# A two-layer graph network on one core: a fixed order for the fill, and four steps moved in the turns

## The chip, the core and the metric

The kernel runs on one core of one Trainium2 chip. The metric is the device time of one execution in microseconds (us); lower is better. Before the change it is 2993.7 us, the median of three runs (2993.65 to 2993.97).

The engines are called PE (TensorE matmuls), PEld (TensorE weight loads), DVE (VectorE), ACT (ScalarE), POOL (GpSimd) and SP (SyncE, which here only issues DMAs).

## The reference

64 graphs of 256 nodes with 256 features go through two layers. All is float32; `adj` is a 0/1 integer matrix.

```python
# layer 0
def _gat(h, adj, W, a, out_features):
    Wh = jnp.matmul(h, W)
    e = leaky_relu(Wh @ a[:out] + swapaxes(Wh @ a[out:], 1, 2), 0.2)
    att = softmax(where(adj > 0, e, NEG), axis=1)
    return att @ Wh
h = _gat(_gat(x, adj, W1, a1, F), adj, W2, a2, F)
h = _layernorm(x + h, g_ln1, b_ln1)
x = _layernorm(h + relu(h @ w_ff1 + b_ff1) @ w_ff2 + b_ff2, g_ln2, b_ln2)
# layer 1: 8 heads of 32
attn = softmax(q @ k.T / sqrt(32), axis=-1)          # q = x Wq + bq, k = x Wk + bk
out = sum(attn * (adj == r) @ (x Wv[r] + bv[r]) for r in range(4))
x = _ln(x + out @ Wo + bo, g1, beta1)
x = _ln(x + gelu(x @ W1 + b1) @ W2 + b2, g2, beta2)
```

## The kernel before

**Units and turns.** A unit is two graphs: 512 rows, held as four blocks of 128. There are 32 units. The main loop (L1566) calls `turn(u, u+1, u+2)` 32 times. A turn works on three units at once: attention and the second feed-forward of unit y (`u`), the first feed-forward of unit x (`u+1`), and both graph attentions of unit z (`u+2`). The steps of the three are interleaved by hand. Turn 30 has no z, turn 31 has neither x nor z. What must exist before turn 0, all of unit 0 up to the end of layer 0 and the graph attentions of unit 1, is made in the fill (L1531 to L1565).

**Order.** `tc.manual_schedule(engines=...)` makes the instructions of the named engines run in the order in which they are written; the scheduler places the others by its own estimate. In the fill that is PE and SP. In a turn (L1263) it is PE, SP, DVE and ACT, in turn 31 only PE and SP. [...]

**Seven products.** Matrix products of two by two blocks are done with seven block products instead of eight, with sums of blocks made before and after. A step name such as `4a` in `hidden_seven` (L870) means product 4 on half a of the hidden features. Products 1, 6, 7, 4 of a half add up in one PSUM bank (`one[h]`), products 2, 5, 3 in another (`two[h]`); after each, `taken` (L907) copies the bank to h1 on ACT if it is the first part of its block, or adds it on DVE (L909). The next product into the bank waits for that. `c`, `d`, `r` and `s` are the activations of finished blocks on ACT; `4` activates its block itself. `HiddenOut` (L959) does the same for the second matrix: `sums` on DVE (L975), `product` on PE (L989), `add` into y on DVE (L997). `Projections` (L1008) does q, k and v.

**Banks.** `bank` gives one of six PSUM banks with the tag g; two more, po and zo, belong to attention.

**Attention.** `scores(n)` makes four banks of scores for one of four quads (graph, half of the heads) and their exponentials on ACT (L1085); `masks(n)` multiplies by the adjacency on DVE (L1089, two instructions of 128x1024), `totals(n)` adds halves on DVE (L1094), `sums(n)` are the products with v (L1104) and of the totals (L1107, zo), `shares(b)` divides.

**Graph attention.** `project` (L1137) makes one 128x260 product a block (`xpp`, L741) and copies it on ACT; `first_scores` and `second_scores` transpose a column into rows (L750); a `Softmax` (L754) has `scores` (ACT L767, then DVE L769), `exp` (ACT L772), `masks` (DVE L776), `shares` and `scaled` (ACT L792). `first_sums` and `second_sums` are the products with the weights (`hpp` L801, `ygp` L812).

**Norms.** `moments` and `norm` take statistics on DVE (L827, L828) and a power on POOL (L838, L839); `offsets` is one small DVE instruction (L846); `applied_norm` runs on ACT (L856); `affine` is two DVE instructions of 128x1024 (L865 times the gain, L868 plus the shift).

**Folding.** `folding` (L624) is a generator that folds gains and shifts of the norms into the next weights: `shifted` (16 one-column products a half, L596), `joined` (four products and two, `pr`, of 512 columns; DVE steps L616 to L622), `scaled` and the sums `seven` and `seven_out` on POOL (L573 to L603). `next(fold)` runs it to its next `yield`.

**Before the fill's block**, the weights are loaded on SP, and three steps wait for such loads: DVE's subtraction on wv (L562), POOL's row additions (L651) and DVE's on brow (L656).

Of the kernel before, what the change touches and what calls it, by code (L numbers as in the profile page):

```python
# [16 lines left out]
P = 128  # L17
# [368 lines left out]
def narrow_path(  # L386
# [172 lines left out]
    wv = const.tile([P, KB, 2, F], F32, name="wv")  # L559
    for r in range(2):  # L560
        nc.sync.dma_start(wv[:, :, r, :], t_Wv[r].rearrange("(c p) f -> p c f", p=P))
    nc.vector.tensor_tensor(wv[:, :, 1, :], wv[:, :, 1, :], wv[:, :, 0, :], ALU.subtract)  # L562
    wvf = wv.rearrange("p c r f -> p c (r f)")
    w1, w2 = weight(t_W1, "w1"), weight(t_W2, "w2")
    rg3, rb3, rg4, rb4 = row(t_g1, "rg3"), row(t_be1, "rb3"), row(t_g2, "rg4"), row(t_be2, "rb4")
# [58 lines left out]
    def folding():  # L624

        shifted(wf1, range(FB // 2), lb1, bf1, "bf1")
        yield
        shifted(wf1, range(FB // 2, FB), lb1, bf1, "bf1")
        scaled(wf1, lg1)
        wf1s.extend(seven(wf1, "wf1"))  # L630
        wf2s.extend(seven_out(wf2, "wf2"))
        yield
        joined(wqk, "wqk", brow[:, 0:2])
        wqks.extend(seven(wqk, "wqk"))
        yield
        joined(wvf, "wv", brow[:, 2:4])
        wvs.extend(seven(wvf, "wv"))
        shifted(w1, range(FB // 2), lb3, b1, "b1")
        yield
        shifted(w1, range(FB // 2, FB), lb3, b1, "b1")  # L640
        scaled(w1, lg3)
        w1s.extend(seven(w1, "w1"))
        w2s.extend(seven_out(w2, "w2"))
        yield
# [2 lines left out]


    rows = work.tile([P, T, 2 * F], F32, tag="v", name="rows", bufs=1)
    for n, (rb, v) in enumerate(((rb1, g_bf2), (rb2, t_bo), (rb3, t_b2))):  # L650
        nc.gpsimd.tensor_add(rb, rb, row(v, None, rows[:, n, :F]))  # L651
# [4 lines left out]
    nc.vector.tensor_tensor(brow[:, 3], brow[:, 3], brow[:, 2], ALU.subtract)  # L656


    mark = {}
# [94 lines left out]
    class Softmax:  # L754

        def __init__(s, u, l, wh, rows, c):
            s.u, s.wh, s.rows, s.c = u, wh, rows, c
            s.s = (work.tile([P, T, N], F32, tag="v", name=f"s{u}_{l}", bufs=1) if u > 1 else
                   work.tile([P, 2 * T, N], F32, tag="e", name=f"s{u}_{l}")[:, :T])
            s.z = work.tile([P, T], F32, tag="z", name=f"z{u}_{l}")  # L760

# [97 lines left out]
    def affine(y, g_, b_):  # L859

        times(y, g_)
        plus(y, b_)
# [355 lines left out]
    def turn(y_, x_, z):  # L1218
# [45 lines left out]
                                            ("PE", "SP", "DVE", "Activation")[:4 if X else 2]})  # L1264
        with order:
            p.sums()
            while late:
                affine(*late.pop(0))
            if X:
                n = X.pop("n")  # L1270
                offsets(*n)
# [44 lines left out]
            if X:  # L1316
                totals(0)
            else:
                with behind("projected"):
                    masks(0)  # L1320
                    totals(0)
            p("v3 q4 v4" if middle else "q4 v4")
            if waiting:
                last = norm(w, 3, wy, mv=last)
# [23 lines left out]
            if not X:  # L1348
                with behind("out"):
                    shares(0)  # L1350
            first("2b ra 1b")
            masks(2, (0,))
            first("7a")
            masks(2, (2,))
            first("5b sa 6b 4a")
            totals(2)
            first("3b rb 7b")
# [43 lines left out]
            if Z:  # L1401
                out(1)
                Z["m"].scores(0)
                Z["m"].scores(1)
                Z["m"].exp(0)
                Z["m"].exp(1)
                out.sums(4)
                offsets(*n)
                out(2)
                applied_norm(y, *n, range(T))  # L1410
                Z["m"].masks(0)
                out(5)
                Z["m"].masks(1)
                Z["m"].shares()
            elif X:
                out.product(5)
                out.sums(3)
                out.add(5)
            if not Z:
                applied_norm(y, *n)  # L1420
            else:
                Z["m"].scaled(WH)
            if Z:
                out.product(6)
                hT = normed_features(y_, 2, y, copied=(1, 2))
                nc.scalar.activation(work.tile([P, 1], F32, tag="ve", name=f"ve{y_}"), mhalf[:, 0:1], AF.Gelu)
                out.add(6)
                out.sums(3)
                out(3)
            elif X:  # L1430
                out(6)
                out.sums(4)
                out(7, 3)
            if not Z:
# [25 lines left out]
            if Z:  # L1460
                second("2a 1a")
                n = norm(x_, 1, X["y"], mv=n, rest=range(NB + 1, T))
                second("2b 1b ca 6a")
                offsets(*n)
                applied_norm(X["y"], *n, [0])
                applied_norm(X["y"], *n, [2, 3], True)
                second("5a")
                applied_norm(X["y"], *n, [1])
                affine(y, rg3, rb3)
                second("6b 5b cb")  # L1470
                X["hT"] = normed_features(x_, 1, X["y"], natural=True)
# [56 lines left out]

    waiting, late = [], []

    with tc.manual_schedule(engines={mybir.EngineType.PE, mybir.EngineType.SP}):  # L1531
        for stage in (early_first, project, first_softmax):
            stage(0)
        early_first(1)
        next(fold)
        for stage in (project, first_softmax):
            stage(1)
        first_sums(0)
        next(fold)
        second_softmax(0)  # L1540
        first_sums(1)
        next(fold)
        second_softmax(1)
        for b in range(G):
            second_sums(0, (b,))
            normed(0, 0, g[0]["y"], range(b * NB, (b + 1) * NB))
        next(fold)
        g[0]["hT"] = to_features(g[0]["y"], "h1T0")
        for u in range(2):
            checked(u, g[u]["aq"])  # L1550
        affine(g[0]["y"], rg1, rb1)
        load_x(2)
        load_rows(2)
        load_adjacency(2)
        first_hidden(0)("2a 1a 2b 1b 5a 5b 3a 3b 6a ra 6b rb 7a sa 7b sb 4a 4b")
        first = HiddenOut(0, 0, g[0]["y"], g[0]["h1"], wf2s, out_sums(0, 0))
        first.sums(1, 2, 4, 3)
        first(1, 2, 5, 6, 3)
        normed(0, 1, g[0]["y"], range(NB))
        first(7, 4)  # L1560
        normed(0, 1, g[0]["y"], range(NB, T))
        g[1]["n"] = norm(1, 0, g[1]["y"], mv=second_sums(1))
        g[0]["hT"] = with_ones(to_features(g[0]["y"], "h2T0", (nc.scalar.copy,) * 2))
        late.append((g[0]["y"], rg2, rb2))
        next(fold)  # L1565
        for u in range(NG):  # L1566
            turn(u, u + 1, u + 2)

# [53 lines left out]
```

## Time and profile before

| | |
|---|---|
| median of three runs | 2993.7 us |
| the profiled execution | 2993.49 us |
| its span, first to last instruction | 2991.8 us |
| PE busy | 2950.5 us (99%), 22192 matmuls |
| DVE busy | 2616.8 us (87%), 5024 instructions |
| ACT busy | 1820.6 us (61%) |
| POOL busy | 624.3 us (21%) |
| HBM traffic | 56.8 MB read, 16.8 MB written |

The execution's time is 1.7 us longer than its span. The page gives, for each engine, busy time, groups of instructions by line, and what ended the idle time before them; a tile's name stands without its number, so `h1a` is `one[h]` and `h1b` is `two[h]` of the hidden products. In the timeline a line starts with the start and the length of an instruction (or of several merged ones, xcount) in us; a bracket at the end gives the idle time of that engine just before it and who ended it. Matmul ends are modelled.

### The profile page before, as it was taken

To read this page: it belongs to the slowest core of one execution; us is meant where nothing else is said; L and a number is where in the kernel's file an instruction comes from. 1 tells how busy PE (TensorE), PEld (TensorE's weight loads), DVE (VectorE), ACT (ScalarE), POOL (GpSimd) and SP (SyncE) were. 2 spreads that over 40 slices of the span, in tenths; PEclk is the share of its full clock that TensorE was granted. 3 is DMA by queue.
4 is the path that set the end of the run, shared out by engine and by line. 5 is a ranking of instruction groups with operands and counts; after the bars stand their busy time and mean duration, and the time that the engine had idled before them with its cause. 6 is when DMAs were issued, how large, how long until landed. Compare 5 with 4: busy or idle time off the path is not lost.

```text
span 2991.8 us, 58459 instructions
## 1 busy us (share of the span) xinstructions
PE 2950.5 (99%) x22192; PEld 2494.1 (83%) x22192; DVE 2616.8 (87%) x5024; ACT 1820.6 (61%) x3803; POOL 624.3 (21%) x930
## 2 busy tenths in 40 slices
PE   7999999999999999999999999999999999999998
PEld 5788888888888888888888888888888888888876
DVE  5789989889898889898889898898988898988887
ACT  4466656656655666666666566566566666666653
POOL 4222111221211221211221112212112212112211
PEclk8999999999999999999999999999999999999999
DMA  5011111111111111111111111111111111111000
GB/s 150 13 29 36 34 36 26 42 34 36 33 31 33 42 34 36 30 27 40 36 37 34 35 26 42 35 37 34 31 33 42 34 36 31 26 40 35 18 11 16
DMA packets 416883, 105.36 MB, mean 35 GB/s; under 512 B 360746, under 2 KB 416084, under 8 KB 416596
## 3 DMA queue, kind: packets, MB, share of 16 engines
q1 hardware_dynamic: 415196, 100.23, 15.3%
q8 instruction: 177, 2.90, 0.4%
q0 software_dynamic: 1056, 1.05, 0.1%
q14 instruction: 110, 0.90, 0.1%
q10 hardware_dynamic: 344, 0.28, 0.0%
HBM read 56.78 MB, written 16.78 MB: 25 GB/s over the span
## 4 chain that ended last, share of the span: by engine, by line
PE 95%; DVE 2%; DMA 1%; ACT 1%; POOL 0%; issue 0%; SPq 0%; DVEq 0%; POOLq 0%; ACTq 0%
PE yf L989 26%; PE h1a L900 15%; PE h1b L900 11%; PE po L1104 8%; PE v L1056 7%; PE qk L1056 6%; PE sp L1076 5%; PE xpp L741 4%; PE yop L812 4%; PE hpp L801 3%; PE ygp L812 3%; PE zo L1107 2%; PE rows L750 1%; DVE st L827 0%; DMA wf<-in_L_gnn_w_ff_dram 0%
## 5 line engine op out<-in xcount | busy, mean ns | idle before, releaser
L1089 DVE TENSOR_TENSOR ea<-e,aT 128x1024 f32<-128x1024 f32 x256 | 307.5, 1213 | 2.8 <-ACT e L1085 2.8
L856 ACT ACTIVATE y<-y,nm,rs 128x256 f32<-128x256 f32 x450 | 242.7, 593 | 95.5 <-DVE nm L846 89.2
L912 ACT COPY h<-h1b 128x512 f32<-128x512 f32 x262 | 153.0, 584 | 223.1 <-PE h1b L900 221.4
L1085 ACT ACTIVATE e<-sp 128x512 f32<-128x512 f32 x512 | 270.8, 598 | 27.4 <-PE sp L1076 20.7
L1043 ACT COPY qk<-qk 128x512 f32<-128x512 f32 x128 | 74.5, 582 | 290.1 <-PE qk L1056 290.1
L918 ACT ACTIVATE h<-h,cols 128x256 f32<-128x256 f32 x512 | 221.7, 501 | 38.5 <-DVE h L909 38.5
L711 POOL COPY hT<-yt 32x256 f32<-32x256 f32 x244 | 211.7, 867 | 139.5 <-DVE yt L694 131.7
L909 DVE TENSOR_TENSOR h<-h1a,h 128x512 f32<-128x512 f32 x262 | 176.1, 681 | 68.3 <-PE h1a L900 64.0
L838 POOL TENSOR_SCALAR rs<-mv 128x4 f32<-128x4 f32 (+1 forms) x134 | 34.2, 255 | 897.8 <-DVE mv L828 480.1
L827 DVE BATCH_NORM_STATS2 st<-y 128x6 f32<-128x256 f32 x512 | 208.0, 408 | 5.6
L997 DVE TENSOR_TENSOR y<-yf,y 128x256 f32<-128x256 f32 x448 | 184.8, 413 | 25.5 <-PE yf L989 25.4
L1117 POOL TENSOR_TENSOR low<-low,rq 128x16 f32<-128x16 f32 x64 | 14.0, 219 | 806.9 <-DVE rq L1116 806.9
L868 DVE TENSOR_TENSOR y<-y,rb 128x1024 f32<-128x1024 f32 (+1 forms) x130 | 167.0, 1285 | 3.2
L743 ACT COPY xp<-xpp 128x260 f32<-128x260 f32 x128 | 45.5, 387 | 194.2 <-PE xpp L741 194.1
L865 DVE TENSOR_TENSOR y<-y,rg 128x1024 f32<-128x1024 f32 (+1 forms) x130 | 155.7, 1198 | 1.2 <-ACT y L856 1.1
L1094 DVE TENSOR_TENSOR es<-e 128x1024 f32<-128x1024 f32 x128 | 155.6, 1216 | 0.0
L839 POOL TENSOR_TENSOR rs<-rs,mhalf 128x4 f32<-128x4 f32 (+1 forms) x134 | 146.2, 1091 | 8.3
L1076 PE MATMUL sp<-qk 32*128 32x256 f32 x2048 | 146.6, 400 | 0.0
L1104 PE MATMUL po<-e,v 128*32 128x256 f32 x2048 | 136.3, 384 | 0.0
L900 PE MATMUL h1a<-tt,wf 128*128 128x256 f32 x512 | 134.5, 386 | 0.3 <-DVE h L909 0.3
L1104 PE MATMUL po<-ea,v 128*32 128x256 f32 x2048 | 134.3, 379 | 0.0
L741 PE MATMUL xpp<-gwe,xT 128*128 128x260 f32 x512 | 128.0, 394 | 2.8 <-ACT xT L675 2.8
(284 smaller groups left out, 7744.3 us busy)
## 6 DMA issues: line engine op xcount, KB each, us to landing
hT<-yt SPq DMA_DIRECT2D x852, 32.0 KB, 1.9
y<-in_x_dram SPq DMA_DIRECT2D x32, 512.0 KB, 4.5
xq<-in_x_dram SPq DMA_DIRECT2D x240, 64.0 KB, 2.2
aq<-in_adj_dram SPq DMA_DIRECT2D x240, 64.0 KB, 2.4
out_dram<-y SPq DMA_DIRECT2D x30, 512.0 KB, 2.8
wf<-in_L_gnn_w_ff_dram SPq DMA_DIRECT2D x2, 1024.0 KB, 7.4
w<-in_L_gnn_W_dram SPq DMA_DIRECT2D x2, 1024.0 KB, 7.6
first<-in_adj_dram POOLq DMA_DIRECT2D x2, 512.0 KB, 7.8
```

The lines of the kernel that those rows point to most:

```text
L711: nc.gpsimd.tensor_copy(to, at)
L741: nc.tensor.matmul(ps[:, :WX], hT[k][:, t * P:(t + 1) * P], gwe[:, k, :], start=(k == 0), stop=(k == KB - 1))
L812: nc.tensor.matmul(ps[:, i * F:(i + 1) * F], lhs(t, k), rhs(b, k), start=(k == 0), stop=(k == n - 1))
L856: mark["normed"] = nc.scalar.activation(y[:, t, :], y[:, t, :], AF.Identity, bias=nm[:, t:t + 1], scale=rs[:, t:t + 1])
L900: nc.tensor.matmul(ps[:, i * N:(i + 1) * N], w_[:, f * P:(f + 1) * P], m, start=first and i == 0, stop=True, skip_group_check=True)
L918: nc.scalar.activation(y, y if ps is None else ps[:, i * N:(i + 1) * N], func, bias=bi[:, f:f + 1])
L989: nc.tensor.matmul(s.ps[n][:, i * F2:(i + 1) * F2], a[:, k, i * P:(i + 1) * P], w_[:, k, :], start=n in (1, 2, 5) and i == 0 and k == 0, s ...
L1056: nc.tensor.matmul(ps[:, i * N:(i + 1) * N], l, r, start=n in (1, 2, 5) and i == 0, stop=True, skip_group_check=True)
L1076: nc.tensor.matmul(ps[a][:, j * N:(j + 1) * N], k_[hp, m, j0:j0 + P], q[hp, m, b * N:(b + 1) * N], start=True, stop=True)
L1085: nc.scalar.activation(e[:, a, :], ps[a], AF.Exp, scale=isd)
L1089: nc.vector.tensor_tensor(ea[:, a:a + 2, :], e[:, a:a + 2, :], ab[:, None, :].to_broadcast([P, 2, NB * N]), ALU.mult)
L1104: nc.tensor.matmul(po[hp, m * N:(m + 1) * N], vs[:, hp], w[:, a, j * N:(j + 1) * N], start=(n == 0), stop=(n == len(terms) - 1))
```

## The change

**Fill.** The block now orders all five engines. The order in it is new: unit 0's first softmax is complete before unit 1's adjacency and features are used; unit 0's second scores and softmax come right after its first sums; unit 1's projection, first softmax and the folding are set between. Unit 1's second softmax moves into the steps of unit 0's first hidden product. `checked` of unit 0 comes earlier. The folding has its yields elsewhere: both halves of `shifted` go together, and `seven_out` of wf2, `joined` of wqk, `seven` of wqk with `joined` of wv, and `seven` of wv are steps of their own. The three steps ahead of the block (wv, brow, the row additions) move into it. Unit 1's second scores get a buffer with the tag q. The scheme of norms splits: statistics first, `applied_norm` later.

**Turns.** The affine steps in `late` (turn 0: one; turn 31: two) move from the start of the turn to after `totals(0)`. `masks(2)`, which was two halves around step 7a, comes whole after 7a (turns 0 to 30). In turn 30, `out(6)` moves ahead of `applied_norm`, and the affine step and the store of the waiting unit move from before the second hidden product to after its steps 5a and 5b.

```diff
-    nc.vector.tensor_tensor(wv[:, :, 1, :], wv[:, :, 1, :], wv[:, :, 0, :], ALU.subtract)
...
     def folding():
         shifted(wf1, range(FB // 2), lb1, bf1, "bf1")
-        yield
         shifted(wf1, range(FB // 2, FB), lb1, bf1, "bf1")
         scaled(wf1, lg1)
         wf1s.extend(seven(wf1, "wf1"))
+        yield
         wf2s.extend(seven_out(wf2, "wf2"))
         yield
         joined(wqk, "wqk", brow[:, 0:2])
+        yield
         wqks.extend(seven(wqk, "wqk"))
+        nc.vector.tensor_tensor(brow[:, 3], brow[:, 3], brow[:, 2], ALU.subtract)
+        nc.vector.tensor_tensor(wv[:, :, 1, :], wv[:, :, 1, :], wv[:, :, 0, :], ALU.subtract)
+        joined(wvf, "wv", brow[:, 2:4])
         yield
-        joined(wvf, "wv", brow[:, 2:4])
+        for rb, v in shifts:
+            nc.gpsimd.tensor_add(rb, rb, v)
         wvs.extend(seven(wvf, "wv"))
+        yield
         shifted(w1, range(FB // 2), lb3, b1, "b1")
-        yield
         shifted(w1, range(FB // 2, FB), lb3, b1, "b1")
...
-            s.s = (work.tile([P, T, N], F32, tag="v", name=f"s{u}_{l}", bufs=1) if u > 1 else
+            s.s = (work.tile([P, T, N], F32, tag="v" if u > 1 else "q", name=f"s{u}_{l}", bufs=1)
+                   if u > 1 or u + l == 2 else
...
             p.sums()
-            while late:
-                affine(*late.pop(0))
...
                     totals(0)
+            while late:
+                affine(*late.pop(0))
             p("v3 q4 v4" if middle else "q4 v4")
...
-            first("2b ra 1b")
-            masks(2, (0,))
-            first("7a")
-            masks(2, (2,))
+            first("2b ra 1b 7a")
+            masks(2)
             first("5b sa 6b 4a")
...
+            if X and not Z:
+                out(6)
             if not Z:
                 applied_norm(y, *n)
...
             elif X:
-                out(6)
                 out.sums(4)
...
-            if waiting:
+            if waiting and Z:
                 affine(waiting[0][1], rg4, rb4)
                 stored(*waiting.pop(), slice(0, T))
...
                 second("5a 5b")
+                if waiting:
+                    affine(waiting[0][1], rg4, rb4)
+                    stored(*waiting.pop(), slice(0, T))
...
-    with tc.manual_schedule(engines={mybir.EngineType.PE, mybir.EngineType.SP}):
+    with tc.manual_schedule(engines={getattr(mybir.EngineType, n) for n in
+                                     ("PE", "SP", "DVE", "Activation", "Pool")}):
+        a, b = g[0], g[1]
...
+        early_first(0)
+        project(0)
+        first_scores(0)
+        spread(a["m"])
+        powers(a["m"])
+        early_first(1)
+        shared(a["m"])
+        a["m"].scaled(WH)
+        checked(0, a["aq"])
+        next(fold)
+        first_sums(0)
+        project(1, range(NB))
+        second_scores(0)
+        project(1, range(NB, T))
+        spread(a["m"])
+        powers(a["m"])
+        first_scores(1)
+        spread(b["m"])
+        shared(a["m"])
+        a["m"].scaled(F)
+        powers(b["m"])
+        next(fold)
+        next(fold)
+        shared(b["m"])
+        b["m"].scaled(WH)
+        parts = []
+        for k in range(G):
+            second_sums(0, (k,))
+            parts.append(norm(0, 0, a["y"], range(k * NB, (k + 1) * NB)))
+        first_sums(1)
+        next(fold)
+        for n in parts:
+            applied_norm(a["y"], *n)
+        checked(1, b["aq"])
+        a["hT"] = to_features(a["y"], "h1T0")
+        next(fold)
...
+        steps = first_hidden(0)
+        steps("2a 1a 2b 1b")
+        second_scores(1)
+        spread(b["m"])
+        next(fold)
+        steps("5a 5b")
+        powers(b["m"])
+        affine(a["y"], rg1, rb1)
+        steps("3a 3b")
+        shared(b["m"])
+        steps("6a ra 6b rb")
+        b["m"].scaled(F)
+        steps("7a sa 7b sb 4a 4b")
...
+        first(7)
+        applied_norm(a["y"], *n)
+        first(4)
+        n = norm(0, 1, a["y"], range(NB, T))
+        mv = second_sums(1)
+        applied_norm(a["y"], *n)
+        b["n"] = norm(1, 0, b["y"], mv=mv)
+        a["hT"] = with_ones(to_features(a["y"], "h2T0", (nc.scalar.copy,) * 2))
+        late.append((a["y"], rg2, rb2))
```

Here `spread` is `m.scores(0), m.scores(1)`, `powers` is `m.exp(0), m.exp(1)`, and `shared` is `m.masks(0), m.masks(1), m.shares()`.

More of the change, by code (lines that the diff above doesn't have):

```diff
@@ L649, in narrow_path @@
     rows = work.tile([P, T, 2 * F], F32, tag="v", name="rows", bufs=1)
-    for n, (rb, v) in enumerate(((rb1, g_bf2), (rb2, t_bo), (rb3, t_b2))):
-        nc.gpsimd.tensor_add(rb, rb, row(v, None, rows[:, n, :F]))
+    shifts = [(rb, row(v, None, rows[:, n, :F]))
+              for n, (rb, v) in enumerate(((rb1, g_bf2), (rb2, t_bo), (rb3, t_b2)))]
     brow = rows[one, :, F:]
@@ L655, in narrow_path @@
     nc.sync.dma_start(brow[:, 2:4], t_bv[0:2].rearrange("(o r) f -> o r f", o=1))
-    nc.vector.tensor_tensor(brow[:, 3], brow[:, 3], brow[:, 2], ALU.subtract)
     mark = {}
@@ L1529, in narrow_path, with spread, powers, shared @@
     waiting, late = [], []
-    with tc.manual_schedule(engines={mybir.EngineType.PE, mybir.EngineType.SP}):
-        for stage in (early_first, project, first_softmax):
-            stage(0)
+    with tc.manual_schedule(engines={getattr(mybir.EngineType, n) for n in
+                                     ("PE", "SP", "DVE", "Activation", "Pool")}):
+        a, b = g[0], g[1]
+        def spread(m):
+            m.scores(0)
+            m.scores(1)
+        def powers(m):
+            m.exp(0)
+            m.exp(1)
+        def shared(m):
+            m.masks(0)
+            m.masks(1)
+            m.shares()
+        early_first(0)
[3 more added lines that the diff above has]
+        powers(a["m"])
         early_first(1)
+        shared(a["m"])
+        a["m"].scaled(WH)
+        checked(0, a["aq"])
         next(fold)
-        for stage in (project, first_softmax):
-            stage(1)
         first_sums(0)
-        next(fold)
-        second_softmax(0)
+        project(1, range(NB))
[8 more added lines that the diff above has]
+        powers(b["m"])
+        next(fold)
+        next(fold)
[5 more added lines that the diff above has]
+            parts.append(norm(0, 0, a["y"], range(k * NB, (k + 1) * NB)))
         first_sums(1)
         next(fold)
[L1543 to L1546, printed above, removed]
+        for n in parts:
+            applied_norm(a["y"], *n)
+        checked(1, b["aq"])
+        a["hT"] = to_features(a["y"], "h1T0")
         next(fold)
[L1548 to L1551, printed above, removed]
         load_x(2)
@@ L1554, in narrow_path @@
         load_adjacency(2)
-        first_hidden(0)("2a 1a 2b 1b 5a 5b 3a 3b 6a ra 6b rb 7a sa 7b sb 4a 4b")
-        first = HiddenOut(0, 0, g[0]["y"], g[0]["h1"], wf2s, out_sums(0, 0))
+        steps = first_hidden(0)
[11 more added lines that the diff above has]
+        steps("7a sa 7b sb 4a 4b")
+        first = HiddenOut(0, 0, a["y"], a["h1"], wf2s, out_sums(0, 0))
         first.sums(1, 2, 4, 3)
         first(1, 2, 5, 6, 3)
[L1559 to L1565, printed above, removed]
+        n = norm(0, 1, a["y"], range(NB))
+        first(7)
[7 more added lines that the diff above has]
+        late.append((a["y"], rg2, rb2))
+    with tc.manual_schedule(engines={mybir.EngineType.PE, mybir.EngineType.SP}):
         for u in range(NG):
```

## The prediction, made before the changed kernel was seen

> **What bounds the kernel now.** I read the page's chain of waits first, then the waits of TensorE, then its busy time by stage, and last the timeline of one turn.
>
> ```profile
> PE 95%; DVE 2%; DMA 1%; ACT 1%; POOL 0%; issue 0%; SPq 0%; DVEq 0%; POOLq 0%; ACTq 0%
> ```
>
> ```profile
> 0.00:112.00 112.00, 89.98 (x447) 73.29 (x447) 61.55 (x141) 46.67 (x100) 42.67 (x55) 0.89 0.36 100
> 112.00:2863.00 2751.00, 2750.59 (x20856) 2331.18 (x20857) 2458.43 (x4708) 1722.49 (x3603) 567.28 (x848) 1.00 0.16 34
> 2863.00:2991.80 128.80, 109.92 (x891) 89.60 (x889) 96.82 (x177) 51.42 (x102) 14.37 (x28) 0.97 0.04 14
> ```
>
> The numbers before the first brackets are PE's busy us, the third from last the granted clock. TensorE is never idle for long between 112 and 2863 us; only the fill (22 us idle, clock 0.89) and the drain (19 us idle) are open. So the fill's rewrite can win at most some 20 us, and anything that touches the 31 turns with a partner unit counts thirty times. A busy row still hides stalls, so I looked at one turn (29 periods from turn 0 to turn 29 take 2631.9 us, 90.75 each).
>
> ```profile
> 2767.98 0.69 DVE L909 TENSOR_TENSOR h<-h1a,h 128x512 f32<-128x512 f32 x1 [0.62 <-PE h1a L900]
> 2768.59 1.22 DVE L1089 TENSOR_TENSOR ea<-e,aT 128x1024 f32<-128x1024 f32 x1
> 2769.72 0.68 DVE L909 TENSOR_TENSOR h<-h1a,h 128x512 f32<-128x512 f32 x1
> 2770.32 1.22 DVE L1089 TENSOR_TENSOR ea<-e,aT 128x1024 f32<-128x1024 f32 x1
> 2771.45 1.22 DVE L1094 TENSOR_TENSOR es<-e 128x1024 f32<-128x1024 f32 x1
> 2772.59 0.68 DVE L909 TENSOR_TENSOR h<-h1b,h 128x512 f32<-128x512 f32 x1
> ...
> 2769.22 0.84 PEld L900 LDWEIGHTS h1a<-tt,wf1s 128*128 128x128 f32 x4
> 2770.45 0.73 PEld L900 LDWEIGHTS h1a<-tt,wf 128*128 128x128 f32 x4 [0.40 <-DVE h L909]
> 2771.21 0.84 PEld L900 LDWEIGHTS h1b<-hT,wf1s 128*128 128x128 f32 x4
> ```
>
> Here step 4a loads its weights 0.40 us late, because the addition of step 7a (2769.72) stands behind half a mask (2768.59) on VectorE. A group of four normally takes 0.864 us (the chain of waits gives 1.73 for eight); from 6b to 3b two groups take 2771.21 - 2769.22 = 1.99 us, so the stall costs 1.99 - 1.73 = 0.26 us.
>
> A second wait in the same turn shows no loss at all, but is at its limit:
>
> ```profile
> 2773.30 1.33 ACT L943 ACTIVATE h<-h,cols 128x512 f32<-128x512 f32 x2 [0.75 <-DVE h L909]
> 2774.55 0.58 ACT L1085 ACTIVATE e<-sp 128x512 f32<-128x512 f32 x1
> ...
> 2775.17 0.19 PEld L741 LDWEIGHTS xpp<-gwe,xT 128*128 128x128 f32 x1
> ```
>
> The line at 2775.17 is the first load of the second projection block (`project`, t=1). It starts 0.05 us after the first exponential of `scores(3)` ends (2775.12). The g tag has six banks: four hold `scores(3)`, one the open product of half b, one the first projection block; the second block needs the bank that the first exponential frees. That exponential stands behind `rb` (L943), which waits for 3b's addition (2772.59).
>
> **The Trainium skill.** "TensorE: Matmul & The Clock Gate", Architectural detail, says that TensorE's queue pulls weight loads ahead of running matmuls, while ScalarE and VectorE are strictly first in, first out. The trace agrees: the load at 2775.17 was 0.09 us behind its place (4 x 0.219 after 2774.32 + 0.11 for the cold first) and cost nothing. After the stall at 2770.45 the next group came 0.76 instead of 0.864 later: a load may be about 0.11 us late for free. The same page, Part 1 (What's actually happening), says TensorE falls to half clock after about 3.4 us of little activity; here the clock was 0.50 from 62.7 to 73.0 us. "SBUF — State Buffer", Who interferes with whom, has VectorE and GpSimd share a port pair under an exclusive lock: the same addition took 2.02 us at 108.15 beside GpSimd's weight scaling and 1.23 at 2775.21 without.
>
> **The turns: one edit.** `masks(2)` whole after 7a. Nothing is added or removed; VectorE's order becomes 1b, 7a, mask, mask, totals, 3b, 7b.
> - 7a's addition is ready when 7a's last matmul ends, 2768.73, plus 0.04 as for 7b: 2768.77. It ends by 2769.5, 4a's load is due at 2770.08: the stall goes, -0.26 us.
> - VectorE is free after 1b's addition at 2768.59 and now waits to 2768.77: 0.18 us that the half mask used to fill. Everything behind it in order (masks, totals, 3b's addition, then `rb` and the exponentials on ScalarE) is 0.18 later: the first exponential ends at 2775.31, the second block's load starts at 2775.36. Its place, 0.26 earlier now, is 2774.82. The load is 0.54 late, 0.11 of it free; its matmul starts at 2775.36 + 0.11 = 2775.46 instead of 2775.30.
> - Net +0.16 us a turn, in the 30 turns that project a third unit: **+4.9 us**. If 7a's addition has a second wait in front (1b's started 0.11 after its matmul, not 0.04), +0.23 a turn, +7.0 in all. If the bank isn't the limit, -0.26 a turn, -8 in all.
>
> After 2775.46 nothing waits: VectorE catches up before 7b (3b's addition then ends at 2773.4), so masks(3) is 0.03 later against a TensorE that is 0.16 later.
>
> **The fill, laid out queue by queue with durations of the trace** (scores 0.39 a row, L769 0.65, exponential 0.63, L776 0.35, scaling 0.42, projection or aggregation block 0.86, `joined` 1.73 + 0.86, one `shifted` 1.84; GpSimd 1.27 a fold operation).
> - Gains: VectorE no longer stands 6.5 us at the wv transfer (L562), so the first softmax's exponentials start at 23.0, not 24.98; unit 0's second softmax starts at about 37.4 instead of 42.25. `h1T0` follows at about 61.5, and 2a at about 64.7 instead of 67.55: -2.8 us at that point.
> - Losses inside that stretch: unit 0's masks are queued behind unit 1's L769, and `joined`'s small product behind both; TensorE stands from about 39.5 to 44.4 and goes cold. Unit 0's offsets stand behind wv's folding on VectorE, to 60.4. GpSimd, in order too, holds wf2's folding back for unit 0's second shares (34 to 44) and then runs it beside unit 1's masks, which I lengthen by 1 us; the three row additions (1.0 each) come at about 58, long before their first use at 75. Unit 1's second scores, now in tag q, are free again after its `ygp`, before turn 0's first copy. SP's order is the same, and no DMA is added.
> - Afterwards: before, 2a to turn 0's q5 took 111.96 - 67.55 = 44.4 us. Now 0.44 (rows of unit 1) and one more `shifted` (1.84) stand in it, and two `shifted` in a row are 3.7 us of one-column matmuls, after which I take the clock as halved for 5a to 3a (+2.5). ScalarE must do unit 1's exponentials before 3a's copy, and its four scalings (1.7) before sa, sb and the ends of 4a and 4b; these end at about 90, so yf2 starts there, 1.8 us idle behind yf1. The last offset of unit 0 stands behind the second `ygp` addition. Turn 0's q1 starts at about 108.0 instead of 103.8.
> - Turn 0 gains back: no affine step of 3.2 us (1.25 + 1.94) and no slow L846 (1.22) ahead of q's addition, so q5 doesn't wait (2.83 before), and GpSimd's folding is done. Four steps are 3.45 warm, 4.7 cold: q5 at 111.5 to 112.7, against 111.96. The moved affine step delays unit 1's differences by 1.6 us; 1.7 us of gaps before 1b's addition (1.10 + 0.62) take that up.
>
> Sum for the fill: **+0.4 us**, from -3 (clock stays up, no port conflicts) to +4 (masks and affine steps each locked out by GpSimd).
>
> **The drain, turn 30.**
>
> ```profile
> PE yf L989 <- DVE y L997: 3.5, 3, 1.5
> PE h1b L900 <- DVE tt L882: 1.4, 1, 1.4
> PE h1a L900 <- DVE h L909: 0.9, 2, 0.8
> ```
>
> `out(6)` ahead of the norm: its addition goes at 2882.1 instead of 2882.62, behind no offset that waits for GpSimd: -0.5. The affine step of the waiting unit leaves the queue ahead of the differences (tt): the 1.4 us wait and its 0.1 restart go. The offsets come earlier too, so 3a's copy isn't behind a late norm on ScalarE: most of the 0.8 goes, as does part of ScalarE's tail, which turn 31's first copies wait for (2908.47). The 4a gain of this turn is nothing, since zo waits for totals(3) there. Its store is some 5 us later, last on SP until the outputs of turn 31, with a free y buffer meanwhile, so no one waits. The two late steps in turn 31 are not in a fixed order there; I price them at 0 (-0.5 to +1), under VectorE's 2.8 us gap at 2914. Sum **-3.2**, from -4.5 to -1.
>
> **Sum.** 4.9 + 0.4 - 3.2 = +2.1 us on the profiled execution's 2993.49 (span 2991.8 and 1.7 around it): 2995.6; the median shown is 2993.7, so 2996.
>
> **Rivals.**
> - The bank isn't the limit (0.10): another bank is free for the second block. For it: the wait costs nothing today. Against: it follows the exponential's end by 0.05 us, and I count no seventh bank. -8 + 0.4 - 3.2: 2983.
> - The fill works as meant (0.15): TensorE stays warm, gaps are filled, -6 instead of +0.4: 2989.
> - Slower (0.20): the fixed order in the fill. ScalarE's queue from 5a to 4b holds unit 1's exponentials and scalings ahead of the copies and activations that free TensorE's banks; each further microsecond there is one at q1. It costs +6 to +8 instead of +0.4: about 3001. It decides from a fill later by 4.3 us.
>
> **Numbers.** A measurement of this kernel can tell about 0.2% (6.0 us) from no change. The likeliest case (0.55) runs from 2991 to 3000. Range 2988 to 3002: below lie the first rival and the tail of the second (0.13), above the tail of the third (0.07). Faster by over 0.2%: 0.10 + 0.04; slower: most of the third and a tail of the likeliest, 0.23; the rest, 0.63, within.
>
> **What would show it.** 4a's load without a wait in each turn, and a new one of about 0.5 us on L741 behind the exponential, with turns of 90.9 us: right; turns of 90.5: the first rival. q5 of turn 0 near 112 and TensorE idle behind yf1 near 88 to 90 show the fill; tt without a wait in turn 30 shows the drain. A fill outside -3 to +4, or turns other than 90.9, would make it wrong.

## The result and the profile after

The changed kernel takes 3002.1 us, the median of 12 runs (2999.24 to 3003.2), beside 2994.5 us for the kernel before in the same session: a ratio of 1.0022, 95% interval 1.0013 to 1.0031. That is 6 us more than the 2996 of the prediction and just above the upper end of its range (3002). By the medians the change costs 7.6 us, by the ratio 6.6, where the prediction had +2.3 on its base of 2993.7.

The profiled execution took 2999.24 us, the shortest of the 12; its span is 2997.6 us against 2991.8 before, +5.8 us. I profiled the same kernel once more (run e11); that execution has a span of 3001.1 us and stands for the longer runs. The table cuts the traces at the first q matmul of each turn, all in us.

| | before | predicted change | after | after, again |
|---|---|---|---|---|
| turn 0 starts (q1) | 103.78 | +4.2 | 110.36 | 112.52 |
| turn 0 lasts | 96.15 | -3.6 | 91.84 | 91.85 |
| turns 1 to 29 last | 2631.88 | +4.7 | 2636.09 | 2636.24 |
| of these an undisturbed turn | 90.73 | +0.16 | 90.90 | 90.90 |
| turn 30 lasts | 73.46 | -3.2 | 72.50 | 74.18 |
| turn 31 to the end | 86.57 | 0 | 86.80 | 86.30 |

Both are executions at the short end of their kernel's runs. Four differences of the first profile make up its +5.8: fill and turn 0 +2.27 (q1 6.58 later, turn 0 4.31 shorter), the turns +4.21 (29 times 0.17, less 0.6 for two turns of the trace before that were 0.3 us longer than the others), turn 30 -0.96, the end +0.23.

The chain of waits and the busy time by stage of the changed kernel:

```profile
PE 89%; DVE 7%; ACT 2%; issue 2%; POOL 0%; DMA 0%; ACTq 0%; DVEq 0%; POOLq 0%
```

```profile
0.00:112.00 112.00, 88.49 (x438) 71.70 (x439) 57.70 (x135) 45.16 (x97) 44.33 (x57) 0.89 0.35 100
112.00:2863.00 2751.00, 2745.96 (x20838) 2329.16 (x20837) 2457.28 (x4707) 1715.31 (x3597) 566.14 (x845) 1.00 0.16 34
```

VectorE's part of the chain rose from 2% to 7%: each turn now hangs on an exponential that follows VectorE's masks and additions (in e12 below, without that wait, it is 2% again). PE is busy for 2745.96 of 2751 us in the middle; it was 2750.59. The missing 4.6 us have one name among TensorE's waits over the whole span:

```profile
PE h1a L904 <- DVE h L913: 5.9, 3, 3.7
PE xpp L744 <- ACT e L1089: 5.0, 30, 0.2
```

The second line is the wait that the prediction named, thirty times 0.17 us; the three waits of the first lie in the fill (3.7) and in turn 30. The turn that was shown before, in the changed kernel:

```profile
2774.28 0.69 DVE L913 TENSOR_TENSOR h<-h1a,h 128x512 f32<-128x512 f32 x1 [0.62 <-PE h1a L904]
2775.08 0.69 DVE L913 TENSOR_TENSOR h<-h1a,h 128x512 f32<-128x512 f32 x1
2775.68 1.22 DVE L1093 TENSOR_TENSOR ea<-e,aT 128x1024 f32<-128x1024 f32 x1
...
2776.39 0.84 PEld L904 LDWEIGHTS h1a<-tt,wf 128*128 128x128 f32 x4
...
2781.05 0.57 ACT L1089 ACTIVATE e<-sp 128x512 f32<-128x512 f32 x1
...
2781.67 0.30 PEld L744 LDWEIGHTS xpp<-gwe,xT 128*128 128x128 f32 x2 [0.57 <-ACT e L1089]
```

7a's addition (2775.08) now stands ahead of the mask, and 4a's load (2776.39) has no bracket any more: that stall is gone. The first exponential of `scores(3)` ends at 2781.62, the second block's load starts 0.05 us behind it, and its bracket gives 0.57 us of idle time. Some 0.03 of that lies between any two groups of loads (as in e12 below), so the load is 0.54 us late.

### The profile page after: what moved, and what is told of

It reads as the page before. It is cut to its first block, busy times and chain, and to the rows that moved or that the text cites. A ratio compares the mean times of both kernels' runs of the same rounds, so it can differ in the third digit from the quotient of the medians.

```text
span 2997.6 us, 58472 instructions
## 1 busy us (share of the span) xinstructions
PE 2950.6 (98%) x22192; PEld 2496.0 (83%) x22192; DVE 2617.6 (87%) x5024; ACT 1816.1 (61%) x3803; POOL 624.8 (21%) x930
## 4 chain that ended last, share of the span: by engine, by line
PE 89%; DVE 7%; ACT 2%; issue 2%; POOL 0%; DMA 0%; ACTq 0%; DVEq 0%; POOLq 0%
PE yf L993 26%; PE h1a L904 12%; PE h1b L904 9%; PE po L1108 8%; PE v L1060 7%; PE qk L1060 6%; PE hpp L805 4%; PE yop L816 4%; PE ygp L816 4%; PE sp L1080 3%; PE xpp L744 3%; DVE ea L1093 2%; PE zo L1111 2%; DVE h L913 2%; PE rows L753 1%
```

## The experiments

Each is an edit of the kernel before or of the changed one; every run has a profile and a ratio to the kernel before. The stages of all of them, cut as above:

| run | q1 | turn 0 | a turn | turn 30 | turn 31 | span | ratio to before, 95% |
|---|---|---|---|---|---|---|---|
| before | 103.78 | 96.15 | 90.73 | 73.46 | 86.57 | 2991.8 | |
| e1 | 104.08 | 96.34 | 90.90 | 73.48 | 87.10 | 2997.6 | 1.0015 (1.0008 to 1.0021) |
| e2 | 110.42 | 91.68 | 90.73 | 72.48 | 86.55 | 2992.3 | 1.0003 (0.9995 to 1.0011) |
| e3 | 103.61 | 95.91 | 90.47 | 73.47 | 86.57 | 2983.5 | 0.9973 (0.9963 to 0.9984) |
| e12 | 110.92 | 91.41 | 90.47 | 74.08 | 86.33 | 2986.5 | 0.9979 (0.9971 to 0.9987) |
| e4 | 108.01 | 96.56 | 90.90 | 72.50 | 86.87 | 3000.3 | 1.0022 (1.0013 to 1.0031) |
| e5 | 107.64 | 91.85 | 90.90 | 74.17 | 86.27 | 2996.0 | 1.0012 (1.0004 to 1.0020) |
| e6 | 103.55 | 92.74 | 90.73 | 73.46 | 86.66 | 2988.1 | 0.9985 (0.9978 to 0.9991) |
| e7 | 103.67 | 98.51 | 90.73 | 72.99 | 86.63 | 2993.7 | 0.9997 (0.9988 to 1.0005) |
| e8 | 103.91 | 92.49 | 90.47 | 70.42 | 92.28 | 2983.0 | 0.9961 (0.9948 to 0.9975) |
| e9 | 103.18 | 93.08 | 90.47 | 70.42 | 86.36 | 2976.8 | 0.9948 (0.9935 to 0.9962) |
| e10 | 107.02 | 93.01 | 90.47 | 70.42 | 86.16 | 2980.2 | 0.9954 (0.9940 to 0.9968) |

### The turns: e1, e2, e3 and e12

e1 makes the one edit of the turn alone, in the kernel before:

```diff
-            first("2b ra 1b")
-            masks(2, (0,))
-            first("7a")
-            masks(2, (2,))
+            first("2b ra 1b 7a")
+            masks(2)
```

> The kernel before with one edit, the whole of masks(2) behind step 7a. Bank theory: 4a's stall of 0.26 us goes, the second projection block waits for the first exponential of scores(3), a turn takes 90.90 us instead of 90.73, in 30 turns +5.1 us against before; fill and drain as before. Rival, the longer turn of the changed kernel comes from the state that its fill leaves (buffers, order of the DMAs): turns of 90.73, no change. Rival, the bank is no limit: turns of 90.47, -7.8 us.

Turns of 90.90 us, a span 5.7 us longer and a median 4.4 us longer (2999.21 against 2994.83): the edit alone brings the whole loss of the turns, with the old fill and the old drain around it, and TensorE waits thirty times for the exponential, 5.2 us in all. Both rivals fall.

e2 is the reverse edit in the changed kernel.

> The changed kernel with the old order of masks(2), half of it ahead of step 7a. Bank theory: turns of 90.73 us again, -5 us against the changed kernel, and what is left against before is the fill (+2.3 at the end of turn 0) and the drain (-1.0), so +1 us against before. Rival, the turn was lengthened by something else in the change: turns stay at 90.90, +5.8 us against before.

Turns of 90.73. What is left of the change is a span of 2992.3, +0.5 us (turn 0 ends at 202.10, +2.17, and turn 30 is 0.98 shorter), and a median 1.2 us longer (2996.03 against 2994.83), which its interval doesn't tell from no change. The turns' cost is wholly in this edit.

e3 asks whether the bank is the cause. It keeps the edit and lets the second projection block need its bank one step later:

```diff
-                project(z, range(0, T // 2))
+                project(z, (0,))
             first("4b")
+            if Z:
+                project(z, (1,))
```

> The kernel before with masks(2) behind step 7a and the second projection block behind step 4b instead of ahead of it, so that it needs its bank 0.86 us later. Bank theory: the exponential has ended by then, only the 4a stall is removed, turns of 90.47 us, -7.8 us against before. Rival, the wait moves on to the next thing (step 4b itself waits for 7b's addition, or sums(2) or masks(3) for the later exponentials): turns of 90.7 to 90.9, 0 to +5 us.

Turns of 90.47, so 4a's 0.26 us are now a gain and nothing takes their place; 7.8 us were expected against before, the median is 7.76 us lower (2987.07 against 2994.83). So it was the place of this block that made it wait; it doesn't read what the exponential writes, and by the program the bank is what joins the two. e12 makes the same edit in the changed kernel.

> The changed kernel with one edit: the second projection block behind step 4b. Bank theory: turns of 90.47 instead of 90.90, 0.43 in each of 30 turns, -12.9 us against the changed kernel, the span about 2984.7, -7 us against before. Rival, in the changed kernel another wait (its xpp copy on ScalarE behind 4b's activations) takes the bank's place: turns of 90.7, -6 us.

Turns of 90.47 there too, -0.43 each. The loads of the two blocks in e12:

```profile
2768.59 0.74 PEld L744 LDWEIGHTS xpp<-gwe,xT 128*128 128x128 f32 x4 [0.33 <-issue]
2769.36 0.84 PEld L904 LDWEIGHTS h1a<-tt,wf 128*128 128x128 f32 x4
2770.22 0.84 PEld L744 LDWEIGHTS xpp<-gwe,xT 128*128 128x128 f32 x4
```

The second block's load (2770.22) follows 4b's (2769.36) with no wait for the exponential. One line of order makes the same edit cost 5 us or gain 8.

### The fill: e4, e5 and e6

In the changed kernel q1 came at 110.36, where 108.0 was predicted. Its timeline at that place:

```profile
76.07 1.95 DVE L872 TENSOR_TENSOR y<-y,rb 128x1024 f32<-128x1024 f32 x1
77.94 1.49 DVE L780 SCALAR_TENSOR_TENSOR s<-s,aT 128x256 f32<-128x256 f32 x1
...
83.78 1.27 DVE L913 TENSOR_TENSOR h<-h1a,h 128x512 f32<-128x512 f32 x2
...
80.64 1.32 POOL L574 TENSOR_TENSOR w1s<-w,w1s 128x512 f32<-128x512 f32 x1
81.92 1.44 POOL L575 TENSOR_TENSOR w<-w 128x512 f32<-128x512 f32 x1
...
84.60 5.38 PE L904 MATMUL h1a<-tt,wf 128*128 128x256 f32 x16 [3.73 <-DVE h L913]
```

The four masks of unit 1's second softmax (L780, from 77.94 to 83.65) take 1.48 us each beside GpSimd's folding of w1, and 6a's addition (83.78) is queued behind them, so TensorE stands for 3.73 us. e4 moves the GpSimd operations away, to the end of the fill:

```diff
+        yield
         scaled(w1, lg3)
         w1s.extend(seven(w1, "w1"))
...
         late.append((a["y"], rg2, rb2))
+        next(fold)
```

> The changed kernel with GpSimd's ten operations on w1 and w2 moved from the middle of the fill to its end, the rest unchanged. Port theory: the four masks of the partner unit take 0.35 to 0.42 us each instead of 1.48, the two affine operations 1.22 instead of 1.96, TensorE no longer stands 3.7 us for 6a's addition, q1 of turn 0 at about 106.6 instead of 110.4 us; turn 0 then has the folding beside its first additions and gives back about 1.5 us, so -2 us against the changed kernel. Rival, the masks are slow for another reason (their operands, the read of the accumulator): they stay at 1.48 and q1 at 110.4, no change.

```profile
79.49 0.42 DVE L781 SCALAR_TENSOR_TENSOR s<-s,aT 128x256 f32<-128x256 f32 x1 [2.15 <-ACT s L777]
...
81.42 0.69 DVE L914 TENSOR_TENSOR h<-h1a,h 128x512 f32<-128x512 f32 x1 [0.25 <-PE h1a L905]
...
124.39 4.50 POOL L715 COPY hT<-yt 32x256 f32<-32x256 f32 x4
...
128.94 1.13 PE L905 MATMUL h1b<-hT,wf 128*128 128x256 f32 x4 [2.60 <-POOL hT L715]
```

A mask takes 0.42 us, 6a's addition starts as soon as its matmul has ended, and q1 comes at 108.01. So the slow masks come from GpSimd's work beside them, as the lock would have it. But the gain (2.35 us at q1) was smaller than expected, since a stretch of halved clock lay beside it (the 8 matmuls of step 5 took 3.76 us instead of 2.68), and turn 0 gave back 4.72 us where I had expected 1.5: the folding now runs from 109 to 124 us, and in GpSimd's queue its copies of unit 1's features (124.39) wait behind it; step 2a stands 2.60 us for them, and a half-clock stretch from 130.2 to 133.6 us follows right behind. The span is 2.7 us longer than in the first profile of the changed kernel, but that was the shortest of its runs: the medians, 3001.76 and 3002.14, and the ratios show no difference. The folding at the end wins nothing.

e5 leaves the folding where it is and moves the masks out of its way, behind additions of the output product:

```diff
-        shared(b["m"])
         steps("6a ra 6b rb")
-        b["m"].scaled(F)
...
-        first(1, 2, 5, 6, 3)
+        first(1, 2, 5)
+        b["m"].masks(0)
+        first(6)
+        b["m"].masks(1)
+        b["m"].shares()
+        b["m"].scaled(F)
+        first(3)
```

> The changed kernel with the second masks of unit 1 (and the four scalings after them) moved in the fill from between steps 3b and 6a to between the additions of the output product of unit 0; GpSimd's folding stays where it is. Queue theory: 6a's addition is no longer behind slow masks, TensorE doesn't stand 3.7 us there, q1 of turn 0 at about 108.0 instead of 110.4 us as with the folding at the end, but turn 0 keeps its 91.84: -2.3 us against the changed kernel. Rival, 6a's addition is itself slowed by GpSimd (1.5 us each instead of 0.69) and the stall is only spread over 6a to 7b: q1 at 110, no change.

q1 comes at 107.64 and turn 0 keeps its 91.85: the queue theory holds, and turn 0 ends 2.7 us earlier than in the changed kernel. (Turn 30 was 1.67 longer in this trace; e11 explains why.) Its timeline shows who GpSimd locks out and who not:

```profile
81.18 0.69 DVE L913 TENSOR_TENSOR h<-h1a,h 128x512 f32<-128x512 f32 x1 [0.17 <-PE h1a L904]
...
86.99 2.17 DVE L979 TENSOR_TENSOR eq<-eq,h 128x1024 f32<-128x1024 f32 x1
89.27 2.10 DVE L979 TENSOR_TENSOR eaq<-h,eq 128x1024 f32<-128x1024 f32 x1
...
92.99 2.02 PE L993 MATMUL yf<-wf2t,eq 128*128 128x128 f32 x16 [2.60 <-DVE y L1001]
```

The additions of the hidden product, which take one operand from PSUM, need 0.69 us with GpSimd busy as without. The sums of the output product, both operands in SBUF, need up to 2.17 us instead of 1.22, and the next wait (2.60) is already there: the output additions are queued behind four sums, three of them slowed. The Trainium skill, "SBUF — State Buffer", Who interferes with whom, says that a VectorE instruction with two SBUF inputs contends with a GpSimd instruction that reads SBUF, and one with at most one SBUF input, outside the modes that use both ports, doesn't. The durations here agree on both halves of that.

e6 takes the late affine step of turn 0 alone, in the kernel before:

```diff
             p.sums()
-            while late:
-                affine(*late.pop(0))
...
+            while late:
+                affine(*late.pop(0))
             p("v3 q4 v4" if middle else "q4 v4")
```

> The kernel before with the late affine step alone moved behind totals(0). As predicted: q5 of turn 0 doesn't wait 2.83 us for q's addition, turn 0 takes about 93.3 us instead of 96.15, and turn 31 is unchanged: -2.8 us against before. Rival: GpSimd's queue still holds the folding ahead of its copies of unit 1's features, as in the kernel with the folding at the end, and the first step of unit 1 (2a) waits for them instead: turn 0 stays at 95.5 to 96.5, no change.

Turn 0 takes 92.74 us, -3.41, turn 31 is as before, and the median is 2990.15 against 2995.0. The wait of q5 before, and in e6:

```profile
PE qk L1056 <- DVE qk L1040: 2.8, 1, 2.8
PE qk L1056 <- DVE qk L1040: 0.6, 2, 0.5
```

So most of the 4.31 us that turn 0 won in the changed kernel come from this move of two instructions, which needs no new fill. (The trace before has a half-clock stretch at q1, from 103.7 to 107.1 us, and e6 has none; e9 below, with such a stretch, has 93.08, -3.07.)

### The drain: e7, e8, e9 and e10

e7 makes the move of the waiting unit's affine step alone.

```diff
-            if waiting:
+            if waiting and Z:
                 affine(waiting[0][1], rg4, rb4)
                 stored(*waiting.pop(), slice(0, T))
...
                 second("5a 5b")
+                if waiting:
+                    affine(waiting[0][1], rg4, rb4)
+                    stored(*waiting.pop(), slice(0, T))
```

> The kernel before with the affine step and store of the waiting unit alone moved in turn 30 from ahead of the differences to behind step 5b. As predicted: the 1.4 us wait for the differences and most of the 0.8 us wait go, turn 30 takes 71.3 us instead of 73.46. Rival: the two operations of 1.22 us now stand ahead of the offsets, so the norm on ScalarE and with it 3a's copy and 6a's addition come later, and TensorE waits 2 us for 6a's addition: turn 30 takes 73.4 to 73.6, no change.

Turn 30 takes 72.99 us, -0.47: nearer to the rival than to the prediction. (Turn 0 is 2.36 longer in this trace with nothing changed there; a stretch of halved clock from 110.0 to 116.9 us lies on it.) The changed kernel shows what happens, in turn 30:

```profile
2901.82 1.22 DVE L869 TENSOR_TENSOR y<-y,rg 128x1024 f32<-128x1024 f32 x1
2903.07 1.22 DVE L872 TENSOR_TENSOR y<-y,rb 128x1024 f32<-128x1024 f32 x1
2904.21 0.15 DVE L850 SCALAR_TENSOR_TENSOR nm<-mv,rs 128x4 f32<-128x4 f32 x1
2905.51 0.69 DVE L913 TENSOR_TENSOR h<-h1a,h 128x512 f32<-128x512 f32 x1 [1.14 <-ACT h L916]
...
2904.40 0.60 ACT L860 ACTIVATE y<-y,nm,rs 128x256 f32<-128x256 f32 x1 [3.03 <-DVE nm L850]
2904.91 0.56 ACT L916 COPY h<-h1b 128x512 f32<-128x512 f32 x1
...
2906.25 2.10 PE L904 MATMUL h1a<-tt,w 128*128 128x256 f32 x8 [1.97 <-DVE h L913]
```

The two moved operations (2901.82 to 2904.29) stand ahead of the offsets (2904.21), ScalarE's norm waits 3.03 us for these, 3a's copy is behind the norm, 6a's addition behind the copy, and TensorE stands 1.97 us. The wait for the differences (1.4) is gone and this one (0.8 before) has grown by 1.2.

e8 puts the gains together on the kernel before and holds the waiting unit's affine step and store over to turn 31 (only this part and the late steps' new place are shown):

```diff
+            if waiting and not Z:
+                late.append((waiting[0][1], rg4, rb4))
+                held.append(waiting.pop())
...
+            with ExitStack() if X else behind("projected"):
+                while late:
+                    affine(*late.pop(0))
+                while held:
+                    stored(*held.pop(), slice(0, T))
```

> The kernel before (its fill unchanged) with masks(2) behind 7a and the second projection block behind 4b, the late affine step behind totals(0), out(6) ahead of the norm in turn 30, and the affine step and store of the waiting unit held over to turn 31, where all late affine steps start only behind the last addition of the projections. If the costs are separate: turns of 90.47, turn 30 at 70.9 to 71.4 instead of 73.46, turn 31 shorter by about 1.2 (the wait of step 5 for q's addition goes), in all -11 to -12 us against before, a span of about 2980. Rival, the drain's gains are taken back by the sums of out and the masks of turn 31, which VectorE then does later: a span of 2983.

Turn 30 takes 70.42, -3.04, about what the prediction had asked of the drain. Turn 31 takes 92.28, +5.7: six affine operations of 1.2 us now stand ahead of `scores(1)`'s masks and between them, TensorE waits 3.3 us for these, and a stretch of halved clock (2916.4 to 2923.3) follows. The rival was right in kind.

e9 places the held step behind 7b's addition of turn 31, and the other late steps of that turn behind the first two additions of the projections.

> The kernel before, with its own fill, and the parts that gained: masks(2) behind 7a with the second projection block behind 4b; the late affine step behind totals(0), in turn 31 behind the first two additions of the projections; out(6) ahead of the norm; the affine step and store of the waiting unit held over to turn 31, behind 7b's addition there. If the terms add up: turn 0 ends at 195.9, turns of 90.47, turn 30 about 70.5, turn 31 about 85.4 (its 1.27 us wait gone), a span of 2975 to 2976, -16 us against before. Rival: the held step stands ahead of the last sums of turn 31 and the output product waits for it, turn 31 about 87.5, a span of 2978; or a stretch of halved clock falls into turn 31 as in the last kernel and adds 1.7 to 3.4 us.

Turn 31 takes 86.36, and the kernel 2978.8 us against 2994.05: a ratio of 0.9948, the fastest of all here. Of turn 31's expected 1.2 only 0.2 came; I did not follow where the rest went.

e10 is the same with the new fill, its masks as in e5 and its sums spread between the output additions.

> The changed kernel with the same mended turns and drain, and its fill mended: unit 1's masks between the additions of the output product, and the sums of that product spread between its additions, so that the additions don't wait behind four sums (2.60 us in the kernel with the masks behind). If the port lock and the queue order are what the new fill lost by: q1 of turn 0 at 105 to 105.5, turn 0 ends at about 196.4, a span of about 2976, the same as with the old fill within 1 us. Rival, the new fill order is worth less than the old whatever is mended: turn 0 ends at 198 to 199, a span of 2978 to 2979.

q1 comes at 107.02, turn 0 ends at 200.03 against 196.25 in e9, which is past even the rival's 198 to 199. Spreading the sums did remove the wait (from the first output product to q1 20.61 us instead of 22.77 in e5), but TensorE reached that product 1.54 us later than in e5, behind a half-clock stretch of 6.8 us (72.8 to 79.6; 3.4 in e5), and had another from 106.9 to 110.3 us. So part of the 3.8 us is clock, and this profile is one of the longer of five runs: the medians, 2980.49 and 2978.8, differ by 1.7 us. The new order of the fill has no lead over the old one in any of these runs; by how much it is worse once mended is not shown.

### The spread of the runs: e11

> The changed kernel, unedited, profiled once more: its profiled execution took 2999.24 us, the lowest of its runs, while their median is 3002.1. Clock theory: waits of about 2 us of TensorE (6a in turn 30, the fill's 3.7) bring a stretch of halved clock of 3.4 us or not, by where they fall against the clock's own steps, and one more such stretch costs 1.7 us; a profile near 3001 to 3002 shows one more stretch than the first, with turns of 90.90 as in the first. Rival, the turns themselves vary: a later profile near 3002 has turns longer than 90.90.

The second profile has the same turns, 90.90. It is 3.5 us longer in two places: q1 comes 2.16 later, and turn 30 takes 74.18 instead of 72.50. Busy times by window around turn 30's wait for 6a, first the second profile, then the first (the third number from the end is the granted clock):

```profile
2909.80:2913.20 3.40, 3.40 (x13) 2.94 (x13) 2.05 (x4) 3.39 (x9) 0.00 (x0) 0.50 0.00 0
```

```profile
2906.40:2909.80 3.40, 3.40 (x20) 2.88 (x21) 2.79 (x5) 3.37 (x8) 0.00 (x0) 1.00 0.09 32
```

Behind the same idle stretch of 1.97 us one execution has 3.4 us at half clock and 13 matmuls in that time, the other the full clock and 20. The Trainium skill, "TensorE: Matmul & The Clock Gate", What's actually happening, says that the clock is set by a free-running window of activity of about 3.4 us, so that where it stands differs from run to run. That agrees. Of seven traces with this wait (after, e2, e4, e5, e7, e11, e12), e5, e11 and e12 have the half-clock stretch and the others don't, and turn 30 is 1.6 to 1.7 us longer in those three than in after, e2 and e4. Within each trace the changes of the clock up to there lie whole multiples of 3.41 us apart. In those three the whole wait fell between two such marks, and TensorE was busy for 1.45 of the 3.41 us; in the other four a mark cut the wait in two, and the emptier step still held 1.54 (e2) to 1.80 us (e7) of work. So what looks like chance is where the wait falls against these marks. It also fits the fill's 2.16, where the first half-clock stretch lasts 6.9 us in e11 and 3.4 in the first profile; I did not test that one by itself.

## Why the prediction was right and where not

**The turns: right, in mechanism and in size.** Predicted +0.16, measured +0.17 us a turn. 4a's stall went; the first exponential ends 0.19 later in the turn (0.18 predicted); the load is 0.54 late (0.54), and with 90.47 as the turn without that wait (e3, e12) the lateness costs 0.43, which is 0.54 less the 0.11 that I took as free. e1 and e2 show that no other part of the change touches the turns, e3 and e12 that the wait for the bank is the limit. (Thirty times 0.16 is 4.8, not 4.9.) The rival "the bank isn't the limit" falls.

**The fill: the layout was right up to 2a and at q5, one term was mis-sized.** 2a came at 64.33 (64.7 predicted), unit 0's offsets ended at 60.04 (60.4), TensorE stood 4.6 us from 37.7 to 42.4 for the folding (39.5 to 44.4), q5 followed q1 by 3.72 us (3.45 to 4.7). The term that failed is GpSimd's lock: I had lengthened unit 1's masks of the first softmax by 1 us and those of the second not at all. They took 1.48 instead of 0.42 us, four times, with 6a's addition behind them, and TensorE stood 3.73 us. The trace before already had four masks of 0.93 to 1.49 us (46.44, 54.80, 55.69, 57.50) beside GpSimd's folding. e4, without the lock, has q1 at 108.01 against the 108.0 of the prediction; to the tenth that is luck, as e4 had a longer half-clock stretch than the changed kernel and not the wait behind yf1. I had the case of masks and affine steps locked out as the upper bound, +4, of a range and never asked which TensorE wait stood behind these four masks; at the end of turn 0 it measured +2.27 instead of +0.4 (e2 and e12, with the same fill, +2.17 and +2.40). In e11 it is +4.44, of which 0.17 is the turn's own: outside the -3 to +4 that the prediction gave for the fill. Part of the loss came as clock: the 3.73 us stall was followed by a half-clock stretch from 85.1 to 88.5 us. The wait behind yf1, 1.8 us, that I expected on ScalarE did not appear behind the longer stall; e4, without the stall, shows 0.38 us of it.

**Turn 0: right, but for the most part not the fill's doing.** The 2.83 us wait went as predicted (-4.31 us in the turn, -3.6 predicted), and e6 and e9 show that the moved affine step alone gives 3.41 and 3.07.

**The drain: one step failed.** `out(6)` is worth 0.5 as predicted (e7, without it, 72.99; the changed kernel 72.50). The wait for the differences went. "The offsets come earlier too, so 3a's copy isn't behind a late norm on ScalarE" is the step that failed: I counted the two operations where they left the queue and not where they entered it, ahead of the offsets. The 0.8 us that should have gone became 2.0. Turn 30 gave -0.96 instead of -3.2; e8 and e9, where they enter nowhere in that turn, give -3.04. The late steps in turn 31 were free, as priced.

**The sum.** On the first profile the sum is +5.8 against the +2.1 predicted: the end of turn 0 is 1.7 over (2.27 against 0.4 + 0.16), turn 30 is 2.2 over, the end 0.2, and the turns are 0.5 under because two of the trace before were 0.3 us longer. The median is about 3 us above that profile; e11 shows an execution of that length with two more half-clock stretches, one of them right behind the drain's failed step. I had put a price on the halved clock in the fill and none in the drain. By the medians e1 (+4.4) and e2 (+1.2) account for 5.6 of the 7.6 us; the other 2 are not assigned.

The total came close to the 3001 of the third rival, but not for its reason. It put the loss into the fill, behind ScalarE's queue; the larger part lies in the turns (e1), and what TensorE waited for in the fill was VectorE (3.73 us for `h`). Only in e11 did the fill come near the 4.3 us that the rival asked for.

## What to carry to other kernels

Before a wait is removed, look for the one that starts within a few hundredths of a microsecond of its releaser: it has no cost today and can eat the whole gain tomorrow, and more, and it may take one line (a block behind a step instead of ahead of it) to free it. A step that is moved must be priced at both ends: what was behind it where it leaves, and what is behind it where it enters, on the engines that follow too. When work is put "in the gaps" beside GpSimd, list which VectorE operations read two operands from SBUF, and who is queued behind these.

## What the hardware showed that I had not expected

TensorE's clock can halve after an idle stretch of only 1.97 us, in three of seven traces, and costs 1.6 to 1.7 us each time. The three are those in which the wait lay whole within one of the clock's 3.41 us steps (TensorE busy for 1.45 us of it; 1.54 to 1.80 in the others), so the same two-microsecond wait costs 2 or 3.7 us by where it falls. And the lock by GpSimd's folding cost a VectorE instruction with two operands in SBUF no less when it was short: 1.06 us for a mask (0.42 to 1.48), 0.74 for an affine operation (1.22 to 1.96), 0.9 for a sum (1.22 to 2.1). It is the short instructions, and the queues of many of them, that suffer.
